# Half-size weight sums on VectorE, ordering ties beside the norm, and spare accumulators for the last projection in a two-layer attention kernel

## The chip, the cores and the metric

The kernel runs on one core of one Trainium2 chip. The metric is the device time of one launch in microseconds (us). The work is split over TensorE (PE, matrix products; PEld is its weight load), VectorE (DVE), ScalarE (ACT), GpSimd (POOL) and DMA queues issued by SyncE (SP), ScalarE and GpSimd.

## The reference

The input x has 8 images of 32 x 32 tokens with 512 channels. Two layers follow each other, each on the group-normalised x (32 groups of 16 channels, statistics over all tokens of an image):

```python
# layer 0: 16 heads of 32
x = x + (softmax(q k^T * 32**-0.5) v) @ w_proj + b_proj     # q, k, v = gn(x) @ w_qkv
# layer 1: 4 heads of 128, with relative position logits
x = x + (softmax(q k^T + rel_w(q) + rel_h(q)) v) @ Wo       # q = gn(x) @ Wq / sqrt(128), k, v = gn(x) @ Wk, Wv
```

All is float32.

## The kernel before

**Layout.** Activations are kept transposed: a `block` is 128 partitions x 4 chunks of channels x 1024 tokens (2 MB), and eight of them exist (`BLOCKS = 8`). Finished residuals are put away in device memory (`put_away`, L228) and fetched again (`fetch`, L235), both on SP's queue.

**Products in seven parts.** Each 512 x 512 projection is done by a scheme with seven half-size products in place of eight. It needs half-size sums of the activations (`forming`, L336 on, the instruction at L360: four VectorE additions s1, s2, a21, s4 of 128 x 1024) and half-size sums of the weights. The weights' sums are made once at run time: `Matrix.fetch` (L138) loads a matrix, `add_up` makes four subtractions of 128 x 512 (L152) and stores them (L154). For the first three matrices this is at the start. `other_sums` does it for the other five during the first pass, all with GpSimd, fetch and store on GpSimd's queue too.

`seven` emits, for one unit (half of the output channels), the products in the order 0, 5, 1, 4, 6, 2, 3 (`ORDER`) on three accumulators x, y, z. A product is 8 matmuls in 32-column strips, 16 records in the trace. Between the products stand the snapshots: `p1` (ScalarE, L406), `a` (VectorE, L411, after product 5), `b` (L419, after product 4), `p7` (ScalarE, L425). Each accumulates further in the same PSUM bank, so the next product into y waits until `a` or `b` is read. `begun` and `half_done` hold the last `a` and `b`. Each accumulator is a `bank` (three buffers in PSUM). A sink takes the results: `Plain` writes them, `Onto` adds them to the residual (VectorE L507, with bias L509, and GpSimd L502). The very last projection (`after_last`) uses `two_first` and `five_last` instead: products 0 and 1 of both units, then the forms, then 5, 4, 6, 2, 3 of each unit.

**Attention of layer 0** (`attention_0`): 64 steps per image, each with a front (scores, L603, into the four-bank tile `ps`; exponential on ScalarE, L611, into one of two `e` buffers) and, one step later, a back (values, L622, into `acc`; VectorE adds e to the running sum, L631 for the first two of a group of eight steps, L633 after that). At the end of a group `finish` sums over partitions on TensorE (L643) and `normalise` divides (ScalarE L566, VectorE L568 to L584, GpSimd L588). Layer 1 (`attention_1`) works on tiles of 512 columns from `bank` (L718, L719, L721, L730, L741).

**Norm.** `statistics` makes two bn_stats (L259) per chunk and one bn_aggr (L260), with two buffers `st`; `group_norm` makes a chain of small VectorE instructions (L285 to L296), a power on GpSimd (L300), and one normalising instruction for each of the four chunks (L304). In the first image the statistics read the SBUF copies that ScalarE makes of the transposed input (L837).

**The passes.** For b = 0 to 8 the attention of layer 0 on image b is emitted side by side with a chain of other work: the output projection `after_0` and norm of image b-1, the output projection `after_1` of image b-2, the projections `second` and attention of layer 1 of image b-1, and the load, norm and projections of image b+1. `side_by_side` hands out products by their cost so that both end together; `woven` puts a step of one generator after every so many of another. In b=0 the chain is the rest of image 0's projections woven with the load of image 1, then image 1's projections woven with `other_sums`. In b=1 it begins with `after_0` of image 0; in b=2 to 7 with `after_0`, then `after_1` woven with the norm. Pass b=8 has no layer 0 attention; after it stands `after_last`.

**Order.** The text's order is a priority. The framework lays out each engine's queue by its own plan of when instructions become ready (in the trace, product 6 of the last projection is issued ahead of product 4). `tc.issue_after(i)` forbids the instructions in its block to stand ahead of i in i's engine's queue. Before the change it ties the norm's first instruction behind `half_done` (b=2 on), its L304 behind `begun` (b=1), and the form additions of a loaded image behind `added`, the last sum of layer 1.

## Time and profile before

| | us |
|---|---|
| median of three runs | 3847.89 (3846.76 to 3849.78) |
| the profiled execution's own time | 3848.35 |
| its span in the trace | 3846.6 |
| TensorE busy in the span | 3789.4 |
| VectorE, ScalarE, GpSimd busy | 2555.1, 1760.2, 621.6 |
| mean granted TensorE clock | 0.998 |

A line of the timeline gives start, duration, engine, source line, operation, output and input tiles with their sizes, the number of instructions merged, and in brackets the idle time of the engine ahead of it and what ended that. A line of the waits gives who waited for whom, the total in us, how many times, and the longest. A matmul's end is modelled: where an engine's instructions overlap, their durations may contain waiting.

### The profile page before, as it was taken

The numbers are of one execution on the slowest core, as the hardware profiler recorded it, in microseconds if no ns is written. First come the engines' busy times: TensorE is split into PE (matmuls) and PEld (weight loads), VectorE is DVE, ScalarE is ACT, GpSimd is POOL, SyncE is SP. The second block draws the span as 40 slices with busy tenths as digits, with TensorE's granted clock in tenths as the row PEclk, the third lists the DMA queues.
The fourth block names the chain that finished last, engine by engine and source line by source line (L and its number), as shares of the span: only waits on it lengthen the run. The fifth ranks groups of instructions, "written<-read, shape, count | busy, mean of one in ns | idle before, by whom it ended". The sixth has DMA issues, their size and how long they took to land.

```text
span 3846.6 us, 79883 instructions
## 1 busy us (share of the span) xinstructions
PE 3789.4 (99%) x34478; PEld 1376.3 (36%) x34478; DVE 2555.1 (66%) x2966; ACT 1760.2 (46%) x1830; POOL 621.6 (16%) x398
## 2 busy tenths in 40 slices
PE   9999999999999999999999999999999999999998
PEld 4222244222443234432343323433234332334353
DVE  6777775686755866558665686656866568665544
ACT  3554544545444454444544445444454445553132
POOL 1342101121011211012101121111210112001201
PEclk9999999999999999999999999999999999999999
DMA  6122120142202322023120241103311023110321
GB/s 185 61 88 81 41 59 6 44 122 62 56 9 83 89 54 56 13 92 85 45 55 16 93 93 38 50 21 98 90 40 41 26 96 78 33 37 31 109 41 26
DMA packets 482983, 234.72 MB, mean 61 GB/s; under 512 B 269600, under 2 KB 461376, under 8 KB 481600
## 3 DMA queue, kind: packets, MB, share of 16 engines
q1 hardware_dynamic: 470992, 213.74, 20.5%
q0 software_dynamic: 2608, 13.70, 1.0%
q8 instruction: 273, 4.47, 0.5%
q10 hardware_dynamic: 9024, 2.10, 0.3%
q14 instruction: 86, 0.70, 0.1%
HBM read 170.72 MB, written 58.72 MB: 60 GB/s over the span
## 4 chain that ended last, share of the span: by engine, by line
PE 88%; DVE 7%; ACT 2%; issue 2%; DMA 0%; SPq 0%; POOL 0%; DVEq 0%; ACTq 0%; POOLq 0%
PE ps L603 12%; PE ps L718 11%; PE acc L730 11%; PE acc L622 11%; PE y_q L327 4%; PE y_v L327 4%; PE y_k L327 4%; PE ps L719 3%; PE x_q L327 3%; PE x_v L327 3%; PE z_k L327 3%; PE x_k L327 3%; PE z_q L327 3%; PE z_v L327 3%; DVE es L633 2%; ACT e L611 2%
## 5 line engine op out<-in xcount | busy, mean ns | idle before, releaser
L611 ACT ACTIVATE e<-ps 128x2048 f32<-128x2048 f32 x512 | 961.7, 1878 | 840.1 <-PE ps L603 630.0
L633 DVE TENSOR_TENSOR es<-es,e 128x2048 f32<-128x2048 f32 x384 | 894.8, 2330 | 403.7 <-ACT e L611 400.4
L603 PE MATMUL ps<-q,k 32*64 32x512 f32 x8192 | 579.1, 614 | 17.1 <-ACT e L611 17.1
L622 PE MATMUL acc<-e,v 128*32 128x512 f32 x4096 | 546.7, 605 | 0.0
L721 ACT ACTIVATE e<-ps 128x512 f32<-128x512 f32 x512 | 305.7, 597 | 507.1 <-PE ps L719 436.4
L718 PE MATMUL ps<-q,k 128*128 128x512 f32 x1024 | 525.0, 594 | 0.2 <-DVE posT L704 0.2
L730 PE MATMUL acc<-e,v 128*128 128x512 f32 x1024 | 522.0, 593 | 0.3 <-ACT e L721 0.3
L588 POOL TENSOR_TENSOR q<-q,su 128x512 f32<-128x512 f32 x128 | 212.7, 1662 | 1550.3 <-DVE su L584 1427.7
L741 DVE TENSOR_TENSOR es<-es,e 128x512 f32<-128x512 f32 x384 | 290.4, 756 | 251.0 <-ACT e L721 248.4
L719 PE MATMUL ps<-posT,sel 128*128 128x512 f32 x512 | 406.6, 794 | 0.0
L718 PEld LDWEIGHTS ps<-q,k 128*128 128x128 f32 x1024 | 192.5, 190 | 230.1 <-issue 218.5
L603 PEld LDWEIGHTS ps<-q,k 32*64 32x64 f32 x8192 | 120.6, 130 | 410.1 <-issue 223.5
L730 PEld LDWEIGHTS acc<-e,v 128*128 128x128 f32 x1024 | 193.1, 189 | 147.3 <-issue 92.6
L622 PEld LDWEIGHTS acc<-e,v 128*32 128x32 f32 x4096 | 81.3, 108 | 412.7 <-issue 366.1
L631 DVE TENSOR_TENSOR es<-e,e 128x2048 f32<-128x2048 f32 x64 | 171.6, 2681 | 32.8 <-ACT e L611 32.7
L568 DVE STREAM_TRANSPOSE tu<-su 128x512 f32<-128x512 f32 x128 | 90.5, 707 | 97.3 <-ACT su L566 95.7
L719 PEld LDWEIGHTS ps<-posT,sel 128*128 128x128 f32 x512 | 97.3, 190 | 122.5 <-issue 122.5
L566 ACT COPY su<-sums 128x512 f32<-128x512 f32 x128 | 74.9, 585 | 131.2 <-PE sums L643 81.5
L704 DVE TENSOR_TENSOR posT<-pp,posT 32x512 fp32r<-32x512 f32 x128 | 112.0, 875 | 31.9 <-ACT posT L699 30.6
L492 POOL TENSOR_TENSOR k<-b_k,p_k 128x512 f32<-128x512 f32 x32 | 52.0, 1624 | 483.4 <-ACT p_k L425 472.7
L699 ACT CAST posT<-pp 32x512 fp32r<-32x512 f32 x128 | 105.9, 827 | 45.8 <-PE pp L686 44.7
L492 POOL TENSOR_TENSOR v<-b_v,p_v 128x512 f32<-128x512 f32 x32 | 51.6, 1614 | 433.9 <-ACT p_v L425 433.9
(214 smaller groups left out, 4546.0 us busy)
## 6 DMA issues: line engine op xcount, KB each, us to landing
w_qkv<-ws_qkv SPq DMA_DIRECT2D x168, 128.0 KB, 2.5
d<-x0T SPq DMA_DIRECT2D x32, 512.0 KB, 3.0
x1T<-d SPq DMA_DIRECT2D x32, 512.0 KB, 5.9
d<-x1T SPq DMA_DIRECT2D x32, 512.0 KB, 3.6
x2T<-d SPq DMA_DIRECT2D x32, 512.0 KB, 6.1
w_qkv<-in_L_conv_w_qkv SPq DMA_DIRECT2D x126, 128.0 KB, 2.2
out<-ot SPq DMA_DIRECT2D x240, 64.0 KB, 2.0
xs<-in_x SPq DMA_DIRECT2D x224, 64.0 KB, 2.5
```

Source lines behind the costliest of these rows:

```text
L327: ins = nc.tensor.matmul(out[columns, :], weights[:, columns], moving, start=start, stop=stop, skip_group_check=open_sum,)
L588: nc.gpsimd.tensor_tensor(dst, dst, su, op=ALU.mult)
L603: nc.tensor.matmul(ps[some, r, :], k[m][rows, j * P + 64 * i : j * P + 64 * i + 64], q[m][rows, h * NB : (h + 1) * NB], start=True, stop=True,
L611: nc.scalar.activation(e, ps, AF.Exp, scale=D0 ** -0.5)
L622: nc.tensor.matmul(acc[r * D0 : (r + 1) * D0, :], v[:, j, c0 : c0 + D0], e[:, r, :], start=(j == blocks[0]), stop=(j == blocks[-1]),)
L631: nc.vector.tensor_add(state["esum"], state["first"], e)
L633: nc.vector.tensor_add(state["esum"], state["esum"], e)
L718: nc.tensor.matmul(ps, k[h][:, keys], q[:, h, queries], start=True, stop=False)
L719: nc.tensor.matmul(ps, sel_flat[:, keys], posT[:, h, queries], start=False, stop=True)
L721: nc.scalar.activation(e, ps, AF.Exp, scale=1.0 / math.sqrt(D1))
L730: nc.tensor.matmul(acc, v[:, j, h * D1 : (h + 1) * D1], e, start=(j == 0), stop=(j == NT - 1),)
L741: added[0] = nc.vector.tensor_add(state["esum"], state["esum"], e)
```

## The change

Seven edits. (1) `other_sums` uses VectorE for all four subtractions of each matrix, one step each, each tied behind `summed`, the last sum of layer 0's attention; fetch and store stay on GpSimd's queue; it is woven with every product instead of every seventh. (2) Image 1's load is woven with every product of `rest_of_first` instead of every second, and its forms are tied behind `summed`. (3) Image 0's `after_0` and the last projection run as `in_two_parts`: products 0 and 1 of both units, with the forms woven between them, then the other five of each unit. (4) In the last projection the second unit's accumulators are the tiles `acc` and `ps` that the attention used. (5) Beside `after_1` and the norm (and beside image 0's `after_0`) each sum of layer 0's attention is tied behind `reader`, the last `a` or `b` of `seven`; the norm's L304 are tied behind `summed`. (6) The statistics of the last image's second unit in `after_0` are emitted with the norm, tied behind `begun`. (7) The first image's statistics read the PSUM banks, into one tile `looks` for all eight.

```diff
         def add_up(self, engines, store, keep=False):
+            run(self.adding(engines, store, lambda: last_form[0], keep))
+        def adding(self, engines, store, behind, keep=False):
...
                 engine = engines[i]
-                with tc.issue_after(last_form[0].ins) if engine is nc.vector else nullcontext():
+                with tc.issue_after(behind().ins) if engine is nc.vector else nullcontext():
                     engine.tensor_tensor(sums[:, i], x, y, op=ALU.subtract)
+                yield 0
             d = dram.tile([P, 4, HC, HN], F32, tag="sums", name=f"ws_{self.name}", bufs=8)
...
+    reader = [None]
+    summed = [None]
+    beside_norm = [False]
...
     def by_columns(out, weights, moving, start, stop, open_sum=False):
...
         a = snapshot("es1", f"a_{name}")
-        begun[0] = nc.vector.tensor_add(a, y, p1)
+        reader[0] = begun[0] = nc.vector.tensor_add(a, y, p1)
         sink.early(p1, a)
...
         b = snapshot("es1", f"b_{name}")
-        half_done[0] = nc.vector.tensor_add(b, y, p1)
+        reader[0] = half_done[0] = nc.vector.tensor_add(b, y, p1)
         sink.middle(b)
...
-    def two_first(fs, u, sink, name):
+    def two_first(fs, u, sink, name, bank=bank):
...
         nc.scalar.copy(p1, x)
+        yield HC
         product(x, 1, False)
         sink.c11(x)
+        yield HC
         return p1
-    def five_last(fs, u, sink, name, p1):
+    def five_last(fs, u, sink, name, p1, bank=bank):
         product = taken(fs, u, False)
...
         a = snapshot("es1", f"a_{name}")
-        nc.vector.tensor_add(a, y, p1)
+        begun[0] = nc.vector.tensor_add(a, y, p1)
         sink.early(p1, a)
+        yield HC
         product(y, 4, False)
         b = snapshot("es1", f"b_{name}")
-        nc.vector.tensor_add(b, y, p1)
+        half_done[0] = nc.vector.tensor_add(b, y, p1)
         sink.middle(b)
+        yield HC
         z = bank(f"z_{name}")
...
         nc.scalar.copy(p7, z)
+        yield HC
         product(y, 2, False)
         sink.c12(y, p1)
+        yield HC
         product(z, 3, False)
...
         sink.c22(b, p7)
+        yield HC
+    def in_two_parts(x, m, sinks, name, room=None, done=lambda u: None, behind=None, banks=(bank, bank)):
+        early = [x[:, :HC, :NB], x[:, HC:, :NB]]
+        p1s, fs = [], []
+        def products():
+            for u in range(2):
+                stream.unit(m, False, u)
+                p1s.append((yield from two_first(early, u, sinks[u], f"{name}_{u}", banks[u])))
+        def sums():
+            fs.extend((yield from forming(x, name, room, behind)))
+        yield from woven(products(), sums(), 0, 1)
+        for u in range(2):
+            stream.unit(m, False, u)
+            yield from five_last(fs, u, sinks[u], f"{name}_{u}", p1s[u], banks[u])
+            done(u)
     class Plain:
...
                 state["esum"] = mem.tile([P, HB, NB], F32, tag="es0", name=f"es_{name}", bufs=1)
-                nc.vector.tensor_add(state["esum"], state["first"], e)
+                other = state["first"]
             elif j != blocks[0]:
-                nc.vector.tensor_add(state["esum"], state["esum"], e)
+                other = state["esum"]
+            if j != blocks[0]:
+                with tc.issue_after(reader[0].ins) if beside_norm[0] else nullcontext():
+                    summed[0] = nc.vector.tensor_add(state["esum"], other, e)
             if j != blocks[-1]:
...
         yield from group_norm(st, xT, f"0_{b}")
-        st["xn"] = yield from forming(x, f"xn0_{b}", behind=lambda: added[0])
+        st["xn"] = yield from forming(x, f"xn0_{b}", behind=lambda: added[0] or summed[0])
     def load_first(st):
...
         xT = chunks(x)
+        st["mv"] = small.tile([P, 32], F32, tag="mv", name="mv_0_0", bufs=2)
+        nc.gpsimd.memset(st["mv"], 0.0)
+        looks = small.tile([P, CC, NH, 6], F32, tag="looks", name="looks")
         for h in range(NH):
...
                 nc.scalar.copy(part, banks[cc])
+                nc.vector.bn_stats(looks[:, cc, h, :], banks[cc])
...
             nc.tensor.matmul(idle[:, t % CC, :], ident, rows[:, t, :], start=True, stop=True)
-        for cc in (0, 2, 1, 3):
-            statistics(st, xT, cc, "0_0")
+        for cc in range(CC):
+            nc.vector.bn_aggr(
+                st["mv"][:, : 2 * CC].rearrange("p (s c) -> p c s", c=CC)[:, cc, :],
+                looks[:, cc].rearrange("p h s -> p (h s)"),
+            )
         st["kept"] = put_away(xT, "0_0")
...
     def after_0(b, st, hook=None):
-        fs = st.pop("ao0") if "ao0" in st else forms(st["q0"], f"ao0_{b}", block(f"forms_{b}"))
         x = st["x1"] = block(f"x1T_{b}")
         xT = fetch(st["kept"], x)
+        sinks = [
+            Onto(halves(xT, u), [bproj_sb[:, n * HC + u : n * HC + u + 1] for n in range(2)])
+            for u in range(2)
+        ]
+        def done(u):
+            def look(u=u):
+                for n in range(2):
+                    statistics(st, xT, n * HC + u, f"1_{b}")
+            if b == B - 1 and u:
+                st["look"] = look
+            else:
+                look()
+        if "ao0" not in st:
+            yield from in_two_parts(
+                st["q0"], WP, sinks, f"wp_{b}", block(f"forms_{b}"), done, lambda: summed[0]
+            )
+            return
+        fs = st.pop("ao0")
         for u in range(2):
-            bias = [bproj_sb[:, n * HC + u : n * HC + u + 1] for n in range(2)]
             stream.unit(WP, False, u)
-            yield from seven(
-                fs, u, False, Onto(halves(xT, u), bias), f"wp_{b}_{u}", hook if u else None
-            )
-            for n in range(2):
-                statistics(st, xT, n * HC + u, f"1_{b}")
+            yield from seven(fs, u, False, sinks[u], f"wp_{b}_{u}", hook if u else None)
+            done(u)
     def norm_1(b, st, after=None, behind=None):
         xT = chunks(st["x1"])
+        if "look" in st:
+            with tc.issue_after(begun[0].ins):
+                st.pop("look")()
         st["kept"] = put_away(xT, f"1_{b}")
...
         sinks = [Onto(halves(xT, u), then=put_out(b, st, xT, u)) for u in range(2)]
-        early = [x[:, :HC, :NB], x[:, HC:, :NB]]
-        p1s = []
-        for u in range(2):
-            stream.unit(WO, False, u)
-            p1s.append(two_first(early, u, sinks[u], f"wo_{b}_{u}"))
-        fs = forms(x, f"ao1_{b}")
-        for u in range(2):
-            stream.unit(WO, False, u)
-            five_last(fs, u, sinks[u], f"wo_{b}_{u}", p1s[u])
+        idle = [psum.tile([P, NB], F32, tag="acc", name="wo_acc", bufs=1)]
+        scores = psum.tile([P, HB, NB], F32, tag="ps", name="wo_ps", bufs=1)
+        idle += [scores[:, r, :] for r in range(HB)]
+        run(in_two_parts(x, WO, sinks, f"wo_{b}", banks=(bank, lambda name: idle.pop(0))))
     def woven(main, side, start, gap, places=(0,)):
...
+    def with_norm(part):
+        beside_norm[0] = True
+        yield from part
+        beside_norm[0] = False
     def marked():
...
     def units(m, rows=False):
...
+    def in_parts(m):
+        return [(m, False, u, some) for some in (FIRST_TWO, LAST_FIVE) for u in range(2)]
...
         if b >= 1:
-            plan += units(WP)
+            plan += units(WP) if b > 1 else in_parts(WP)
         if b == 1:
...
             plan += FIRST if b else units(WQ0) + units(WK0)[:1] + units(WV0, True)
-    plan += [(WO, False, u, some) for some in (FIRST_TWO, LAST_FIVE) for u in range(2)]
+    plan += in_parts(WO)
...
     def other_sums():
...
             m.fetch(nc.gpsimd)
-            m.add_up([nc.gpsimd] * 4, nc.gpsimd)
+            yield from m.adding([nc.vector] * 4, nc.gpsimd, lambda: summed[0])
             yield 0
     def at_once(do):
...
             if past is not None:
-                norm = norm_1(b - 1, last, after=lambda: half_done[0])
+                norm = norm_1(
+                    b - 1, last, after=lambda: half_done[0], behind=lambda: summed[0]
+                )
             else:
                 norm = norm_1(b - 1, last, behind=lambda: begun[0])
-            rest.append(after_0(b - 1, last, forms_past if past is not None else None))
+            first = after_0(b - 1, last, forms_past if past is not None else None)
+            rest.append(first if past is not None else with_norm(first))
             total += PRODUCT
             if past is not None:
-                rest.append(woven(later(after_1, b - 2, past), norm, 3, 3))
+                rest.append(with_norm(woven(later(after_1, b - 2, past), norm, 3, 3)))
                 total += PRODUCT
...
         else:
-            rest.append(woven(rest_of_first(here), incoming, 0, 2))
+            rest.append(woven(rest_of_first(here), incoming, 0, 1))
             total += PRODUCT
...
             before = later(before_0, b + 1, coming, forms_0 if last is not None else None)
-            rest.append(before if last is not None else woven(before, other_sums(), 2, 7))
+            rest.append(before if last is not None else woven(before, other_sums(), 2, 1))
             total += 3 * PRODUCT - PRODUCT // 2
```

## The prediction

> **What bounds the kernel now.** I read the page's busy shares first, then who TensorE waited for, then TensorE's gaps in order of time, then the timeline around each gap.
>
> ```profile
> span 3846.6 us, 79883 instructions
> ...
> PE 3789.4 (99%) x34478; PEld 1376.3 (36%) x34478; DVE 2555.1 (66%) x2966; ACT 1760.2 (46%) x1830; POOL 621.6 (16%) x398
> ```
>
> TensorE is the bound; the change removes no matmul, so it can win only TensorE's idle time, 3846.6 - 3789.4 = 57.2 us, and stretches in which its clock was low or a stall hides inside the modelled busy time. The waits of TensorE (us in total, times, longest):
>
> ```profile
> PE ps L603 <- ACT e L611: 17.1, 16, 2.9
> PE y_wo L327 <- DVE a_wo L411: 9.1, 6, 1.8
> ...
> PE x_v L327 <- issue: 3.5, 1, 3.5
> PE sums L643 <- DVE es L633: 3.1, 2, 1.8
> PE y_wp L327 <- DVE forms L360: 2.5, 1, 2.5
> ```
>
> Laid out in time the gaps are: the start 9.0 (4.8 of it the first input); the pass b=0 9.7; b=1 5.4; b=2 to 6 12.35, the same pair (0.98 and 1.42 to 1.77) in each; b=7 2.7; b=8 1.6 and some of 0.3; six of 0.34; the last projection 2.4, and 10.3 after the last matmul. Now one view of each kind. The pair, in b=2:
>
> ```profile
> 843.11 2.98 DVE L304 TENSOR_SCALAR x1T<-x1T,back,rstd 128x1024 f32<-128x1024 f32 x4 [1.20 <-POOL rstd L300]
> 846.01 2.29 DVE L633 TENSOR_TENSOR es<-es,e 128x2048 f32<-128x2048 f32 x1
> 848.38 1.88 ACT L611 ACTIVATE e<-ps 128x2048 f32<-128x2048 f32 x1 [5.25 <-DVE es L633]
> 850.32 1.12 PE L603 MATMUL ps<-q,k 32*64 32x512 f32 x16 [0.98 <-ACT e L611]
> 854.02 4.64 DVE L633 TENSOR_TENSOR es<-es,e 128x2048 f32<-128x2048 f32 x2
> 858.59 0.68 DVE L411 TENSOR_TENSOR a_wo<-y_wo,p_wo 128x512 f32<-128x512 f32 x1
> 859.32 1.92 PE L327 MATMUL y_wo<-f_ao,w_o 128*32 128x512 f32 x16 [1.42 <-DVE a_wo L411]
> ```
>
> Four normalising instructions in a row hold up a sum whose input was there at 839.44. The exponential waits for the sum (two e buffers), TensorE for the exponential. Later two sums in a row stand ahead of the snapshot a_wo, and the product that goes on in the same PSUM bank waits. The weights, in b=0:
>
> ```profile
> 156.08 9.38 DVE L633 TENSOR_TENSOR es<-es,e 128x2048 f32<-128x2048 f32 x2
> 156.23 3.76 POOL L152 TENSOR_TENSOR prep_q<-prep_q 128x512 f32<-128x512 f32 x3
> 165.60 1.07 PE L643 MATMUL sums<-es,ones 128*32 128x512 f32 x8 [1.82 <-DVE es L633]
> 166.59 1.82 PE L603 MATMUL ps<-q,k 32*64 32x512 f32 x16
> ```
>
> Two sums take 9.38 instead of 4.6 while POOL subtracts; TensorE waits 1.82 and then runs slowly (1.82 for 16 matmuls that take 1.11 elsewhere). The opening of b=1, the start, the last projection:
>
> ```profile
> 326.53 2.94 PE L327 MATMUL y_wp<-forms,w_p 128*32 128x512 f32 x16 [2.50 <-DVE forms L360]
> ```
>
> ```profile
> 11.40 1.29 DVE L259 BATCH_NORM_STATS2 st<-x0T 128x6 f32<-128x512 f32 x2 [1.04 <-ACT x0T L837]
> ```
>
> ```profile
> 3820.29 2.33 PE L327 MATMUL y_wo<-f_ao,w_o 128*32 128x512 f32 x17 [1.01 <-DVE a_wo L453]
> 3832.62 1.92 PE L327 MATMUL y_wo<-f_ao,w_o 128*32 128x512 f32 x16
> ```
>
> [...] a sum (two SBUF inputs) has a median of 2.29 and a longest of 6.08, the latter under POOL's subtractions. [...] Here slow matmuls followed gaps of 1.82 and 2.50 already, and not the one of 2.92 at 141.17; I count slow clock only where the trace has it.
>
> **The change part by part.** Times are of the profiled execution: 3848.35 us, span 3846.6, so 1.75 lie around the span. The median of the three runs shown is 3847.89, 0.46 below.
>
> 1. *First statistics.* Now the two `st` buffers let VectorE take only two of the first half's four statistics; it idles 1.04 until 11.40 and ends the eighth at 15.4. With one tile `looks` all four first-half ones (4 x 0.645 from 9.07) end by 11.65, the others by 14.2, four aggregates (0.2 each) by 15.0, against 15.6. [...] The warming matmuls (5.32) start a little later, as VectorE too must leave their bank; they end by 17, before the product, at 18.9. Next comes POOL's power (1.04), unchanged. Bounds: 0 to -2.5 (the latter if TensorE's cold start, 3.46 for a product of 1.9, shortens too). I take **-0.8**.
>
> 2. *Weights.* POOL's 20 subtractions (five matrices, 42 us of POOL with their contention) leave; VectorE gets 20 of 0.68 (its own L152 rows at the start: 0.678 to 0.683), 13.6 us. They lie in VectorE's idle time of about 0.9 ahead of most sums. A late sum costs TensorE nothing up to 2.45 (one ends at 285.51, the exponential that needs its buffer starts at 287.96). That cover is missing at the seven group ends, where the normalising steps and the first sum already leave gaps of 0.6 to 1.5; two or three subtractions will fall there: +1.5. What goes: the 1.82 at 165.60 and the slow stretch behind it (1.82 - 1.11 and 1.94 - 1.06), 3.4 together. The gap of 2.92 at 141.17 comes from the four form additions crowding before L631; they wait for buffers that the previous products hold, so placing their text earlier frees few of them: -0.9. The POOL queue keeps the fetches and stores, each store now behind VectorE; the first reader of a stored sum came 60 us later. Bounds: -8 (all gaps of b=0) to +10 (below). I take **-2.8**.
>
> 3. *Opening of b=1.* Two products of the second unit (2 x 1.72) move ahead of the forms: they fill the 2.50 and spare the cold rows (2.94 - 1.90 and 1.72 - 1.11): -4.1. The order 5, 4 of the last five puts a product right behind the snapshot it waits for (0.69 and perhaps a sum of 2.29 ahead of it); attention steps lie between most: +0.5. Bounds -5.2 to +1. I take **-3.6**. The 1.85 at 376.34 stays: its norm is still behind `begun`.
>
> 4. *Norm beside the last projection, b=2 to 7.* With the normalising instructions tied behind sums, two at most (1.5 us) stand between two sums instead of four (2.98); the exponential of 848.38 then has its buffer in time: 0.98 goes. With sums tied behind the last snapshot, a_wo runs at about 854.3 to 856.4 rather than 858.59, before the 857.9 at which TensorE wanted it: 1.42 goes. Queued behind a waiting sum: a sum tied to `b` may wait about 1.2 more (VectorE stands until 836.55 instead of starting at 835.36), inside the 2.45. The norm ends later by a sum or two, 5 us; its first reader comes at 863, 17 us on. Of 12.35 I take 10.0 and of b=7 1.3 (the 1.31 at 3214.35): **-11.3**. Bounds 0 to -13.9.
>
> 5. *b=8.* The last unit's statistics (four of 0.64, two aggregates) go behind a_wo, which stood behind three of them: the gap of 1.62 goes, save for the residual additions: **-1.5** (0 to -1.6).
>
> 6. *Last projection.* From 3805.24 to 3836.26 lie 31.0 us for 14 products (24.1) and the sums (0.7): 6.2 waste, of which 2.43 shows as gaps; the rest is y_wo waiting for b_wo (3822.97, 3832.57). With the second unit's three accumulators in the attention's free banks its products can fill the first unit's waits. But the framework's plan may still run the units in turn, and outputs bunch at the end (1 MB per unit; the DMA moved 130 to 150 GB/s there). Bounds -6.2 to +1; I take **-3.0**.
>
> Sum: -0.8 - 2.8 - 3.6 - 11.3 - 1.5 - 3.0 = -23.0; 3848.35 - 23.0 = 3825.35, about **3825**.
>
> **Rivals.** (a) *The ties change little*: each only forbids an instruction to come earlier than another, and the norm's gap moves to another sum. For it: the framework lays every queue anew. Against: the tie names just the two pairs that the trace shows late. Term 4 nil: 3825 + 11.3 = 3836. (b) *VectorE stuck behind a fetch*: POOL waited 5.0 to 5.2 for each of three fetches; in VectorE's queue the same wait, less 2.45 of cover, is 2.7 five times: 3825 + 13.5 = 3838.5. Against it: VectorE waits for no DMA anywhere in the trace of before. (c) *Slower: the sums tied behind snapshots.* Four snapshots in each of six passes, 24 places; if at each the exponential chain is held for a product (1.72), TensorE loses 41 and term 4 gives nothing: 3836 + 41 = 3877. It ends slower once each place loses 0.8 (11.7 and the 7.7 of the bound, over 24). Against: the cover of 2.45, and in these passes two products often stand between attention steps, which lengthens it.
>
> **Chances.** A measurement of this kernel can tell about 0.2%, 7.7 us. Forecast 0.62, its own range 3814 to 3834 (all of 4 and 6 won: 3848 - 34; half of 4 and none of 6: 3834); (a) 0.17; (b) 0.12; (c) 0.06; no net change 0.03. Faster (below 3840): 0.62, 0.15 of (a), 0.08 of (b): 0.85. Slower: (c) and a little: 0.07. Same: 0.08. The range 3813 to 3840 holds the forecast and most of (a) and (b).
>
> **What would show it.** In TensorE's waits: a_wo L411 from 9.1 to under 2, L603 on the exponential from 17.1 to about 9, y_wp on the forms gone, sums on es L633 nil; the waits of y_wo at the end shrink, and the last projection takes TensorE some 28 us instead of 31.0. Wrong: VectorE waiting for a prep fetch; new gaps at L603 in b=2 to 7; the second unit's products at the end still in turn.

## The result, and the profile after

| | before | after |
|---|---|---|
| median | 3848.07 us (3846.54 to 3850.42, 22 runs) | 3854.30 us (3852.28 to 3855.52, 22 runs) |
| ratio after/before | | 1.0016, 95% interval 1.0010 to 1.0021 |
| profiled execution, its span | 3848.35, 3846.6 | 3855.17, 3853.4 |

The forecast was 3825; the kernel became 6.2 us slower. Medians are of fast executions; of the six of e8 below, one that took 5572.67 us at a mean granted clock of 0.65 is left out. The page of the kernel after, span and busy shares:

```profile
span 3853.4 us, 79904 instructions
...
PE 3790.3 (98%) x34478; PEld 1371.9 (36%) x34478; DVE 2573.4 (67%) x2986; ACT 1762.4 (46%) x1830; POOL 609.0 (16%) x378
```

TensorE's matmuls are the same 34478; its idle time is 63.1 us instead of 57.2. The waits of TensorE in the kernel after (us in total, times, longest):

```profile
PE ps L637 <- ACT e L645: 26.0, 22, 4.2
PE idle L883 <- DVE looks L879: 5.5, 1, 5.5
...
PE y_wp L335 <- DVE a_wp L463: 2.6, 2, 1.8
PE y_v L335 <- DVE a_v L419: 2.1, 1, 2.1
...
PE y_k L335 <- DVE b_k L427: 1.5, 1, 1.5
...
PE wo_ps L335 <- DVE x2T L541: 0.8, 1, 0.8
...
PE y_wo L335 <- DVE a_wo L419: 0.7, 1, 0.7
```

The waits for a_wo in passes 2 to 6 are gone as predicted (9.1 to 0.7; of the 9.1, 1.6 lay in b=8, and the 0.7 lies there too). But the scores wait longer for the exponential (17.1 to 26.0), and several waits are new: the warming matmuls wait for the looks (the first image's statistics), y_v at the start, y_k in b=0 and y_wp in the opening of b=1 wait for snapshots, and the tile wo_ps, in which the accumulators y and z of the last projection's second unit are two banks, waits for three different readers. To see where the time went I laid the starts of the same TensorE instruction side by side in both timelines, and took the lengths between them:

| stretch (us) | before | after | kept parts (e11) |
|---|---|---|---|
| start to first score matmul | 60.03 | 62.60 | 59.19 |
| to image 0's x_wp (pass b=0) | 248.50 | 256.08 | 246.87 |
| to second layer's x_q (opening of b=1) | 84.44 | 82.91 | 82.92 |
| to last projection's x_wo (rest of b=1 to b=8) | 3412.27 | 3407.33 | 3407.17 |
| last projection, to the end of its last matmul | 31.02 | 34.22 | 31.03 |

So 2.6 are lost at the start, 7.6 in b=0 and 3.2 in the last projection; 1.5 and 4.9 are won between. The last column is explained below. Three stretches of the timeline of the kernel after show the three losses. The start, first before, then after:

```profile
8.45 2.05 ACT L837 COPY x0T<-turned 128x512 f32<-128x512 f32 x4 [4.54 <-PE turned L830]
```

```profile
8.40 0.59 ACT L878 COPY x0T<-turned 128x512 f32<-128x512 f32 x1 [4.46 <-PE turned L871]
9.02 0.70 DVE L879 BATCH_NORM_STATS2 looks<-turned 128x6 f32<-128x512 f32 x1 [4.66 <-ACT x0T L878]
10.70 3.13 ACT L878 COPY x0T<-turned 128x512 f32<-128x512 f32 x6 [1.71 <-PE turned L871]
15.04 0.59 ACT L878 COPY x0T<-turned 128x512 f32<-128x512 f32 x1 [1.21 <-DVE looks L879]
15.65 0.70 DVE L879 BATCH_NORM_STATS2 looks<-turned 128x6 f32<-128x512 f32 x1 [0.27 <-ACT x0T L878]
16.50 7.26 PE L883 MATMUL idle<-x_rows,ident 128*128 128x512 f32 x12 [5.51 <-DVE looks L879]
```

Before, ScalarE copied all four first-half chunks in a row (2.05 us from 8.45). Now it copies one and then stands: each further copy from the same four-bank tile waits until VectorE has looked at the bank before (those at 13.24 and 15.04 start when looks have ended at 13.21 and 15.00), and the queue has copies of the second half, which wait for TensorE until 10.70, in between. The last copy of the tile waits 1.21 for a look, and its own look ends at 16.35; only then can the warming matmuls have the tile. They run at a granted clock of 0.50 until 20.3, and the product x_v starts at 23.69 (19.74 before). The granted clock is 1.00 then and the product takes 1.93 instead of 3.46 (before, it lay mostly in a stretch at 0.50, from 20.09 to 23.51), so that of the 3.9 a loss of 2.6 is left at the first score matmul. Pass b=0:

```profile
256.66 0.58 POOL L158 DMA_DIRECT2D ws_v<-prep_v  x1 [17.67 <-DVE prep_v L155]
261.65 0.59 ACT L516 COPY v<-x_v 128x512 f32<-128x512 f32 x1 [5.38 <-DMA ws_v<-prep_v]
264.07 2.01 PE L637 MATMUL ps<-q,k 32*64 32x512 f32 x16 [4.17 <-ACT e L645]
```

The fourth matrix had its block since 207; its subtractions came one by one until 256.4, its store landed 4.8 us later, and image 1's values need that block. ScalarE stands 5.38 in the copy that writes them, with the exponential queued behind it, and the sixteen matmuls of TensorE after the gap take 2.01 instead of 1.11. Of the 7.6, some 1.7 (an estimate: one spell of 3.41 us at 0.50) are a second fall of the clock, from 146.56 to 149.97. Such a second fall comes only in some executions: the same pass took 254.0 to 255.4 in e1 to e4 and e8, whose edits don't touch it, and 256.7 and 257.0 in e17 and e18. The last projection, second unit:

```profile
3835.81 1.92 PE L335 MATMUL wo_ps<-q,w_o 128*32 128x512 f32 x16 [0.81 <-DVE b_wo L468]
3838.49 1.92 PE L335 MATMUL wo_ps<-f_wo,w_o 128*32 128x512 f32 x16 [0.75 <-ACT p_wo L474]
3841.22 1.92 PE L335 MATMUL wo_ps<-q,w_o 128*32 128x512 f32 x16 [0.81 <-DVE x2T L541]
```

Product 6 (3835.81) writes bank z, and waits for a reader of y; product 2 (3838.49) writes y and waits for a reader of z; product 3 writes z and waits for a reader of y. Before, product 6 ran inside the waits of y.

### The profile page after: what moved, and what is told of

Same layout as the page of the kernel before. It is cut to its first block, busy times and chain, and to the rows that moved or that the text cites. A ratio compares the mean times of both kernels' runs of the same rounds, so it can differ in the third digit from the quotient of the medians.

```text
span 3853.4 us, 79904 instructions
## 1 busy us (share of the span) xinstructions
PE 3790.3 (98%) x34478; PEld 1371.9 (36%) x34478; DVE 2573.4 (67%) x2986; ACT 1762.4 (46%) x1830; POOL 609.0 (16%) x378
## 4 chain that ended last, share of the span: by engine, by line
PE 89%; DVE 7%; ACT 3%; issue 1%; DMA 1%; POOL 0%; SPq 0%; ACTq 0%; DVEq 0%; POOLq 0%
PE ps L637 12%; PE acc L656 11%; PE ps L756 11%; PE acc L768 11%; PE y_k L335 4%; PE y_v L335 4%; PE y_q L335 4%; PE ps L757 3%; PE z_k L335 3%; PE z_q L335 3%; PE x_v L335 3%; PE x_k L335 3%; PE x_q L335 3%; PE z_v L335 3%; DVE es L671 2%; ACT e L645 2%
## 5 line engine op out<-in xcount | busy, mean ns | idle before, releaser
L622 POOL TENSOR_TENSOR q<-q,su 128x512 f32<-128x512 f32 x128 | 200.1, 1563 | 1528.7 <-DVE su L618 1391.6
```

The costliest lines, as they stand in the source:

```text
L622: nc.gpsimd.tensor_tensor(dst, dst, su, op=ALU.mult)
```

## The experiments

Theory: (i) accesses of different engines to different banks of one PSUM tile are made to wait for each other; this costs 2.6 at the start and 3.2 at the end. (ii) A matrix whose sums come late holds a block, and what waits for the block stalls; 6 us in b=0. (iii) Beside the norm VectorE is full, so a wait of TensorE that is taken away there comes back later. Rivals are in each expectation. The kernel before, timed again beside each kernel, took 3847.5 to 3848.0. Where nothing else is said, an experiment is an edit of the changed kernel, called after (3854.3); line numbers in profiles are those of the kernel shown.

**e1, e2: the first statistics.** e1 puts the old code back, e2 is this edit of after:

```diff
-                nc.vector.bn_stats(looks[:, cc, h, :], banks[cc])
+                nc.vector.bn_stats(looks[:, cc, h, :], part)
```

> The changed kernel with only the first statistics put back (read from the SBUF copies, two st buffers). Theory: the copies on ScalarE and the statistics on VectorE take turns on the one four-bank tile, which put the warming matmuls at 16.50 and the first score matmul at 62.60 us instead of 60.03. So the first score matmul comes back to 60.0 and the time is 3854.3 - 2.6 = 3851.7. Rival (a late start is made up later, since the weights and the load of image 1 decide the first pass): first score matmul at 60.0, but 3854.3 all the same.

> The changed kernel with the one tile for all eight looks kept, but each statistic reading the SBUF copy, not the PSUM tile. Theory (the turns on one PSUM tile are the loss, and the two st buffers were a real limit): no turns, the four first-half statistics run in a row, the chain after them starts at about 15.0 instead of 16.63 (15.65 in the kernel before); first score matmul at 59 to 60, time 3851 to 3851.7. Rival (the st buffers were no limit; VectorE is only as early as ScalarE's last copy): the chain starts at 15.6 as in the kernel before, 3851.7. Rival (the reading from PSUM was not the cause): 3854.

Measured: e1 3855.08 (ratio to before 1.0018, 1.0012 to 1.0025), e2 3853.80 (1.0016, 1.0009 to 1.0022). No gain in either median. In the profile of e2 the first score matmul starts at 58.77, earlier than in both kernels, and that execution took 3849.5; in e1's profile it starts at 62.55 although the queues up to there are those of the kernel before, since TensorE ran at a clock of 0.55 from 20 to 30 us (0.83 before). This is taken up again at e13, e17 and e18.

**e3, e4: the last projection.** e3 takes the three common banks for both units (`run(in_two_parts(x, WO, sinks, f"wo_{b}"))`), e4 only separates the tiles:

```diff
         scores = psum.tile([P, HB, NB], F32, tag="ps", name="wo_ps", bufs=1)
-        idle += [scores[:, r, :] for r in range(HB)]
-        run(in_two_parts(x, WO, sinks, f"wo_{b}", banks=(bank, lambda name: idle.pop(0))))
+        idle += [scores[:, 0, :]]
+        run(
+            in_two_parts(
+                x, WO, sinks, f"wo_{b}", banks=(bank, lambda name: idle.pop(0) if idle else bank(name))
+            )
+        )
```

> The changed kernel with the second unit of the last projection back in the three common banks; the generator in two parts stays. Theory: the last projection (first x_wo matmul to the end of the last matmul) takes 31.0 instead of 34.2 us, time 3854.3 - 3.1 = 3851.2. Rival (the new generator's order, not the accumulators, costs the 3.1): 34 us and 3854.

> The changed kernel with the second unit's three accumulators in three different tiles: x in acc, y in one bank of ps, z in a common bank. No accumulator shares a tile with another. Theory (readers and writers of different banks of one tile are made to wait for each other): the product 6 fills the wait for a and the product 3 that for the last addition again; last projection 28 to 31 us, time 3848.5 to 3851.2. Rival (the units standing in turn is what costs, whatever the tiles): 33 to 34 us, about 3854.

Measured: e3 3850.22 (1.0008, 1.0000 to 1.0016), e4 3850.86 (1.0009, 1.0001 to 1.0018); the last projection takes 31.04 in both. In e4's timeline product 6 (z_wo) runs between the matmuls of product 4 again:

```profile
3829.60 0.61 PE L335 MATMUL wo_ps<-f_wo,w_o 128*32 128x512 f32 x3
3830.02 1.46 PE L335 MATMUL z_wo<-q,w_o 128*32 128x512 f32 x10
```

This settles (i) for the end: one tile costs 3.2. It also shows that free accumulators gain nothing over the common banks: the units still stand one after the other, 31.04 against 31.02.

**e5, e6: the weights.** e5 has GpSimd and one matrix per seven products as before; e6 keeps VectorE, with two empty steps after each matrix. First e5, then e6:

```diff
-            yield from m.adding([nc.vector] * 4, nc.gpsimd, lambda: summed[0])
+            m.add_up([nc.gpsimd] * 4, nc.gpsimd)
...
-            rest.append(before if last is not None else woven(before, other_sums(), 2, 1))
+            rest.append(before if last is not None else woven(before, other_sums(), 2, 7))
```

```diff
             yield from m.adding([nc.vector] * 4, nc.gpsimd, lambda: summed[0])
             yield 0
+            yield 0
+            yield 0
```

> The changed kernel with the weights' sums as before: GpSimd subtracts, one matrix after every seventh product. Theory (the new pace lets the fourth matrix take a block ahead of image 1's values, and ScalarE's copy of those waits 5.4 us for its store): the gap of 4.17 at 264 and the slow clock behind it go, the gap of 1.82 and the slow stretch of the kernel before come back at about 165; from the first score matmul to the first x_wp 248.5 to 250 instead of 254.4 to 256.1; time 3854.3 - 6 = 3848.3. Rival (the loss in the first pass lies in the denser load of image 1, which stays): 254 to 256 again, 3854.

> The changed kernel with VectorE still subtracting one by one behind additions, but with two empty steps after each matrix, so that one matrix is fetched per seven products as before, not per five. Theory (the block taken early is the loss, VectorE's subtractions are not): ScalarE waits for no store of weights, no gap of 4 us at 264; first score matmul to first x_wp 248 to 250; time 3854.3 - 6 = 3848.3, equal to GpSimd's version or up to 1.5 below it. Rival (the 13.6 us of subtractions on VectorE are the loss, whatever the pace): 253 to 256, 3852 to 3854, and GpSimd's version faster by 3 or more.

Measured: e5 3848.26 (1.0001, 0.9993 to 1.0010), with 249.56 from the first score matmul to x_wp; e6 3850.73 (1.0007, 0.9999 to 1.0015), with 247.91 there, the shortest so far. So the pace cost, not VectorE's 13.6 us. But e6 loses 3 us in the opening of b=1 (85.93), by the same mechanism one block later. Its timeline:

```profile
326.14 1.27 POOL L536 TENSOR_TENSOR x1T<-x1T,p_wp 128x512 f32<-128x512 f32 x1 [10.34 <-DMA x1T<-d]
328.69 2.28 DVE L368 TENSOR_TENSOR forms<-q 128x1024 f32<-128x1024 f32 x1 [3.26 <-POOL q L622]
338.05 2.02 PE L637 MATMUL ps<-q,k 32*64 32x512 f32 x16 [3.38 <-ACT e L645]
```

and SP's own wait there:

```profile
SPq L239 <- DMA ws_o<-prep_o: 3.6, 1, 3.6
```

The last subtraction of the fifth matrix ran at 314.24, its store was issued at 315.22, and the fetch of x1T, which waited 3.6 for that store, at 319.85. GpSimd's gather (L536, its addition to the residual) waits for the fetch, the division by the sums (L622) stands behind it, the forms behind that, a sum behind the forms. With e15 below this settles (ii).

**e7, e8: the ties.** e7 is the kernel before with the ties of passes 2 to 7 alone (its last projection is written in two parts on the common banks, and takes 31.02 as before); e8 is after without the normalising tie:

```diff
-                norm = norm_1(
-                    b - 1, last, after=lambda: half_done[0], behind=lambda: summed[0]
-                )
+                norm = norm_1(b - 1, last, after=lambda: half_done[0])
```

> The kernel before with the ties beside the norm and the second layer's output projection alone (passes b=2 to 7). The prediction's step 4 gives 3847.6 - 11.3 = 3836.3. Theory now (VectorE has no idle time left in these 40 us, so a wait that is removed comes back at the end of the group; the changed kernel gained 0.9 in each of b=2 to 6): 3847.6 - 4.7 = 3842.9, with a new gap of about 1.3 at the third scores after each pair. Rival (the changed kernel's gain there is owed to other edits, the ties alone give nothing): 3847.6.

> The changed kernel without the tie of the normalising instructions behind the last sum; the sums stay tied behind the snapshots. Theory (VectorE is full here; the order only moves the wait): four normalising instructions in a row again, a gap of about 1 ahead of a score matmul, less of the gap of 1.26 later; each pass within 0.5 of the changed kernel, 3852 to 3856.5. Rival of the prediction (the tie itself removes 0.98 in each pass and costs nothing elsewhere): 0.98 more in each of five or six passes, 3859 to 3860.

Measured: e7 3843.47 (0.9989, 0.9982 to 0.9995), -4.4, as theory (iii) had it and not -11.3. e8 3862.81 (1.0039, 1.0026 to 1.0052; five executions, 3861.67 to 3863.54), 8.5 above after: outside what I expected, on the rival's side. What the tie does is seen in pass b=2; first the kernel after:

```profile
845.48 1.12 PE L637 MATMUL ps<-q,k 32*64 32x512 f32 x16 [0.44 <-ACT e L645]
853.81 1.53 DVE L308 TENSOR_SCALAR x1T<-x1T,back,rstd 128x1024 f32<-128x1024 f32 x2 [0.31 <-POOL rstd L304]
884.59 1.12 PE L637 MATMUL ps<-q,k 32*64 32x512 f32 x16 [1.26 <-ACT e L645]
```

and e8:

```profile
849.94 1.54 DVE L308 TENSOR_SCALAR x1T<-x1T,back,rstd 128x1024 f32<-128x1024 f32 x2 [1.20 <-POOL rstd L304]
883.52 1.12 PE L637 MATMUL ps<-q,k 32*64 32x512 f32 x16 [1.98 <-ACT e L645]
```

In both, one gap of the pair is gone and the other is down to 0.44, and a third has come 40 us later, where the first sum of the next group stands behind four form additions and the division. In after, from 845.1 to 886.8, VectorE is busy for 40.91 of 41.70. The tie lets a sum run while GpSimd makes the power, so VectorE idles 0.31 there, not 1.20: 0.89 won. One pass (from one group end to the same one a pass later) takes 471.2 in before, 470.3 in after and in e7, 471.2 in e8. TensorE won just what VectorE's idle time lost. That is 0.9 in each of five passes. The rest of e8's loss lies elsewhere: pass b=4 takes 472.9 because the clock stood at 0.50 for 3.41 us from 1827.43, behind the same gap of 1.98, and b=7 is 2.4 longer, with a gap of 1.92 ahead of the sums' matmuls that the kernel after has not. Why it comes stays open.

**e9, e10: VectorE's load beside the norm.** Of e7, passes 2 to 8. e9 leaves out two of the four normalising instructions (half the channels stay as they are); e10 gives them to ScalarE:

```diff
+        on_scalar = (1, 3) if behind is not None and after is not None else ()
+        if on_scalar:
+            shift = small.tile([P, CC], F32, tag="shift", name=f"shift_{name}")
+            nc.vector.scalar_tensor_tensor(shift, mean, -1.0, rstd, op0=ALU.mult, op1=ALU.mult)
...
+            if cc in on_scalar:
+                nc.scalar.activation(
+                    xT[cc],
+                    xT[cc],
+                    AF.Identity,
+                    bias=shift[:, cc : cc + 1],
+                    scale=rstd[:, cc : cc + 1],
+                )
+                yield 0
+                continue
```

> The ties alone (3843.5), and in the passes b=2 to 8 two of the four normalising instructions of the second layer's norm are left out: half of its channels stay as they are. This takes 2 x 0.74 us from VectorE in each pass and nothing from TensorE. Theory (VectorE is full for some 40 us beside the norm, 40.9 of 41.7 us busy, so TensorE's gap there is VectorE's work over TensorE's): the gap of 1.25 at the end of the group goes, and about 1.3 in each of b=2 to 7: 3843.5 - 7 = 3836.5. Rival (the gap comes from the order at the end of the group, four form additions ahead of the first sum, whatever went before): the gap stays at 1.25, 3843.

> The ties alone (3843.5), with two of the four normalising instructions of b=2 to 8 moved to ScalarE (scale and bias; one more small instruction on VectorE makes the bias, about 0.2). ScalarE is busy for 19.5 of these 41.6 us. Theory (VectorE is full, ScalarE isn't): VectorE loses 1.3 us, the gap of 1.25 shrinks below 0.3, 3843.5 - 6 = 3837.5. Rival (an instruction of about 1 us on ScalarE stands ahead of an exponential and TensorE waits for that instead): a new gap of about 1 at the scores beside the norm, 3843 to 3849.

Measured: e9 3840.79 (0.9982, 0.9974 to 0.9990), 2.7 below e7, not 7. The timeline of e9, b=2:

```profile
851.21 3.01 DVE L674 TENSOR_TENSOR es<-es,e 128x2048 f32<-128x2048 f32 x1
875.75 1.12 PE L640 MATMUL ps<-q,k 32*64 32x512 f32 x16 [0.90 <-ACT e L648]
```

Of the 1.49 left out, a sum that now falls together with GpSimd's gather took 0.76 back (3.01; 2.25 in e7), and VectorE waited 0.27 for TensorE elsewhere. From the snapshot b to the first sum of the group it took 34.15 instead of 34.52, 0.37 less; TensorE's gap fell by 0.35. So (iii) holds in its exchange of one for one, and my size was wrong: TensorE got back only a part of the work that was taken out of the full queue, 0.35 of 1.49. e10 was slower, 3852.71 (1.0014, 1.0008 to 1.0021), as its rival said. ScalarE's and TensorE's lines in b=2:

```profile
841.68 1.24 ACT L312 ACTIVATE x1T<-x1T,shift,rstd 128x1024 f32<-128x1024 f32 x1 [3.45 <-DVE shift L309]
843.45 1.92 PE L349 MATMUL z_wo<-q,w_o 128*32 128x512 f32 x16 [0.79 <-ACT p_wo L447]
846.35 1.12 PE L651 MATMUL ps<-q,k 32*64 32x512 f32 x16 [0.98 <-ACT e L659]
```

A copy of an accumulator and an exponential stand behind 1.24 each. ScalarE, busy 46% of the span, has no slack at this place. Not all of the loss is ScalarE's: the small VectorE instruction that makes the bias (L309) is not tied, so the sum stands behind it and VectorE idles 1.20 for the power again, which the tie had cut to 0.31. A version with that instruction tied was not run.

**e11, e12: the parts that gained.** e11 is after with e5's weights, the old load of image 1, e2's looks and e4's tiles; e12 adds e10's edit.

> The parts of the change that gained or were mended: the ties, image 0's output projection in two parts, the last image's late statistics, the last projection with three separate tiles, the looks from the SBUF copies; the weights' sums on GpSimd and the load of image 1 as before. If the parts add up as the single runs give them: 3848.3 (the changed kernel with the weights back) - 3.4 (separate tiles) - 0.5 to 2.6 (statistics) = 3842.3 to 3844.4. Rival (the two-part opening of b=1 costs what it gains, and the tie's 0.9 per pass is all there is): equal to the ties alone, 3843.5.

> The same with two of the normalising instructions of b=2 to 8 on ScalarE. Theory: the gains add, 3843.3 - 6 = 3837. Rival (ScalarE is late instead): not below the version without it.

Measured: e11 3839.10 (0.9978, 0.9969 to 0.9987), below both kernels and below what I had added up; e12 3849.07 (1.0004, 0.9996 to 1.0012), 10 worse, as e10 was.

**e13 to e16: one part of the change back into e11.** e13: looks from PSUM; e14: image 1's load with every product (`woven(rest_of_first(here), incoming, 0, 1)` for `0, 2`), its forms tied; e15: VectorE's subtractions, all four in one step at the old pace (`run(m.adding([nc.vector] * 4, ...))`); e16: the old opening of b=1.

> The kept parts (3839.1), with the looks reading the PSUM tiles again, as in the change. Theory (the start costs what the first landmark shows): first score matmul at 62.5 instead of 59.2, 3839.1 + 3.4 = 3842.5. Rival (putting the statistics back into the whole change moved its median by -0.5 and +0.8 only, so the start is made up later): 3839 to 3839.6.

> The kept parts (3839.1) with image 1's load woven with every product and its forms tied behind the last sum, as in the change. Theory (the fall from the changed kernel with the weights back, 3848.3, to the kept parts is 9.2, of which separate tiles give 3.4 and the start 3.4, so 2.4 is the denser load's): first score matmul to first x_wp 249.5 instead of 246.9, 3841.5. Rival (the denser load costs nothing): 3839.

> The kept parts (3839.1), with the four subtractions of each matrix on VectorE, all four in one step at the old pace, tied behind the last sum. Theory (what cost was the block held by a matrix whose sums come late, one by one; GpSimd's contention costs 1 to 2 in the first pass): no wait of 3 us or more for a store of weights, the 1.82 type of gap gone, 3837.5 to 3839. Rival (20 subtractions of 0.68 on VectorE delay its sums, wherever they are put): 3841 to 3845.

> The kept parts (3839.1) with the opening of b=1 as in the kernel before: forms first, then each unit's seven products, no ties there. The prediction's step 3 gives 3839.1 + 3.6 = 3842.7. Theory from the traces (the two gaps of 0.81 and 1.77 behind the snapshots of the second unit take back half): 3839.1 + 1.6 = 3840.7. Rival (nothing): 3839.

| | median us | above e11 | ratio to before | from the landmarks of its profile |
|---|---|---|---|---|
| e13 | 3844.91 | 5.8 | 0.9990 (0.9982 to 0.9999) | start +3.9, b=0 +0.5, b=1 +1.7 |
| e14 | 3841.20 | 2.1 | 0.9983 (0.9977 to 0.9990) | start -0.2, b=0 +1.9, b=1 +1.7 |
| e15 | 3839.99 | 0.9 | 0.9981 (0.9973 to 0.9988) | start -0.5, b=0 +0.7 |
| e16 | 3840.92 | 1.8 | 0.9982 (0.9975 to 0.9989) | b=1 +1.5 |

The statistics do cost: 5.8 against the same looks from the SBUF copies, 3.9 of it at the start. The two-part opening is worth 1.5 to 1.8. VectorE's and GpSimd's sums can't be told apart at the old pace (the 0.9 of e15 lies within the noise), which again says that the pace cost. The +1.7 of e13 and e14 in b=1 is slow clock: the product behind the unchanged gap of 1.77 takes 3.62 and 3.60 instead of 1.92. The denser load came out 2 slower, but how much of that is its own is not shown: it turns the gap of 2.92 into 1.52 (y_k waiting for b_k) and 1.83, and the rest of e14's gaps is one of 1.81 ahead of the sums' matmuls at 166.00, of a kind that comes and goes with the old load too (before has it, e11 has not).

All profiles together show the start better than one or two do. The first score matmul starts at 62.4 to 63.1 in the seven with looks from PSUM (after, e3 to e6, e8, e13), at 60.0 to 61.0 in five of the six with the old statistics (before, e7, e9, e10, e18; the sixth is e1 with 62.55), and at 58.7 to 59.2 in the seven with one tile and SBUF copies (e2, e11, e12, e14 to e17).

**e17, e18: second profiles of e2 and e1.** One run each.

> A second profile of the changed kernel with the looks from the SBUF copies, whose first profile (3849.5) lay 4.3 below its own median (3853.8). Theory (after a gap of 1.8 to 4.2 the clock falls in some executions and not in others): the order and the gaps are the same as in the first profile, and the longer time shows as slow matmuls behind the gaps at 18.5, 141, 258 or 357 us: one or two of the windows there with a granted clock below 0.9 that had 1.00 before. Rival (the time goes into waits, so that a part of the gain is really made up later): longer gaps at full clock.

> A second profile of the changed kernel with the first statistics put back (first profile 3855.8, median 3855.1, lowest 3850.4). Theory: the same gaps; which of the four places runs slowly differs from the first profile (there 20 to 30 us at a clock of 0.50 to 0.59, 3.01 behind the gap of 1.77), and the sum of the slow places accounts for the difference in time to within 1 us. Rival: different gaps.

Measured: 3856.34 and 3856.41. First e2's timeline, then that of e17, the same kernel:

```profile
237.61 1.12 PE L637 MATMUL ps<-q,k 32*64 32x512 f32 x16 [2.02 <-ACT e L645]
357.71 1.92 PE L335 MATMUL y_wp<-forms,w_p 128*32 128x512 f32 x16 [1.77 <-DVE a_wp L463]
```

```profile
237.76 1.91 PE L637 MATMUL ps<-q,k 32*64 32x512 f32 x16 [2.03 <-ACT e L645]
360.51 3.38 PE L335 MATMUL y_wp<-forms,w_p 128*32 128x512 f32 x16 [1.76 <-DVE a_wp L463]
```

The gaps are equal to 0.01; what differs is the matmul behind them. By the landmarks e17 is 2.7 longer in b=0 and 3.3 in b=1, and equal elsewhere to 0.1 (6.1 in all at the last matmul, spans 6.9 apart). e18 keeps e1's gaps too: 2.2 better at the start, 1.5 worse in b=0, 1.7 worse in b=1. So no wait makes the start's gain up again.

The profile's record of the granted clock shows which gap is followed by slow clock. In all 20 profiles, from the first full clock to the last matmul, low clock (0.50) lasts 3.41 us or a multiple of it, and within one execution all such spells start on one grid of 3.413 us: in after at 13.44, 146.56 and 262.61, which are 39 and 34 steps apart. Where the grid lies differs from execution to execution. Below are two grid steps around the gap of 1.77, first of e17, then of e2: the stretch, its length, TensorE's busy time, and, third from the end, the granted clock.

```profile
357.42:360.83 3.41, 1.65 (x14) 0.36 (x14) 3.00 (x4) 0.00 (x0) 0.30 (x1) 1.00 0.54 192
360.83:364.24 3.41, 3.41 (x21) 0.75 (x18) 0.31 (x1) 0.00 (x0) 0.97 (x1) 0.50 0.02 5
```

```profile
353.61:357.02 3.41, 2.34 (x22) 0.33 (x10) 3.34 (x5) 0.60 (x1) 0.00 (x0) 1.00 0.54 189
357.02:360.43 3.41, 2.72 (x26) 0.63 (x26) 1.33 (x3) 0.00 (x0) 1.28 (x1) 1.00 0.03 8
```

In e17 the gap lies whole in one step, and the next step is slow; in e2 an edge of the grid cuts it, and none is. Of the 14 profiles with this gap, the product behind it is slow in five (e1, e13, e14, e17, e18), where the gap lies whole in one step and begins 0.9 us or more into it; it is fast in four where an edge cuts the gap and in five where it begins in the first 0.5 us of a step. Over all 20 profiles, between 25 and 3800 us and outside slow spells, all 21 steps in which TensorE idled 2.0 us or more were followed by a slow one, 12 of the 37 with 1.76 to 2.0, and none with less.

What remains open is why the medians of e1 and e2 hide the start's gain: whether their grid lies badly more often than that of after can't be told from two profiles of each. Warming that runs right up to the first product doesn't decide it, for the product behind 1.77 is fast in e2, e11 and e15 (1.92 in each), which lack it, and slow in e13 (3.62), which has it.

## Why the prediction was wrong, step by step

Terms 1, 2 and 6 came out with the wrong sign, and 3, 4 and 5 gave half of what was forecast or less.

1. *First statistics: forecast -0.8; +2.6 in the profile.* The step "all four first-half ones (4 x 0.645 from 9.07) end by 11.65" failed. It is not the single instruction that failed: the eight that read PSUM in after (L879) took 0.68 to 0.70, the eight that read the SBUF copies in before (L259) 0.64 to 0.70; the step's 0.645 is half of a pair's 1.29. I ordered the copies and looks bank by bank (an assumption; the trace of before has no such pair), while they take turns over the whole four-bank tile: the order is kept between banks of one tile, by waits in the program's own queues (ScalarE 1.21 for a look ahead of the tile's last copy, TensorE 5.51 for the looks ahead of the warming matmuls). I also wrote that the warming matmuls "end by 17, before the product": they ended at 23.7 and the product waited. The part that I credited to the single tile `looks` is real: with looks at the SBUF copies the product x_v starts at 18.48 (e2) and 18.90 (e11), 19.74 before. How much of the loss is the taking of turns, and how much the longer hold on the tile by the looks themselves, is argued from the timeline; a start with a tile for each bank was not run. In the whole change the medians of e1 and e2 show no gain from mending it; only e13 does.
2. *Weights: forecast -2.8; measured +6.0 (after against e5).* The cover "the first reader of a stored sum came 60 us later" was the failed term: I asked who reads the sums, not who wants the block. The bound of +10 held the size. The stall at 165.60 did go in after, but at the old pace VectorE's sums are no faster than GpSimd's (e15). Of the denser load, priced at -0.9 for the crowding near 141, that gap did fall from 2.92 to 1.84; the wait of y_k for b_k (1.52 at 133.10), for which I had no term, took it back.
3. *Opening of b=1: forecast -3.6; -1.5 in the profile, 1.8 in e16.* The mechanism was right, and the wait of y_wp for the forms is gone. The mis-sized term is the order 5, 4, "+0.5": it shows as gaps of 0.81 and 1.77 ahead of y_wp, 2.6 in all, and can cost a slow product besides.
4. *Beside the norm: forecast -11.3; -4.8 in the profile, -4.4 in e7.* The named gaps went (0.98 to 0.44, 1.42 to nothing), and the step that failed is "its first reader comes at 863, 17 us on": I treated the gaps as faults of order with cover behind them. VectorE had no cover; 0.9 in each pass is its idle time of 1.20, which stands in the first line of the pair that I quoted, becoming 0.31, and the rest returned as the gap of 1.26. e7, e8 and e9 agree on this exchange.
5. *b=8: forecast -1.5; measured -0.2* (307.83 to 307.59 from the sums at 3325.63 to x_k). The gap of 1.62 went, but two of 0.47 and 0.69 came some 8 and 12 us later, in the projection's second unit:

```profile
3587.36 1.92 PE L335 MATMUL y_wo<-f_ao,w_o 128*32 128x512 f32 x16 [0.47 <-DVE x2T L541]
3591.69 1.93 PE L335 MATMUL y_wo<-f_ao,w_o 128*32 128x512 f32 x16 [0.69 <-DVE a_wo L419]
```

There a residual addition and the snapshot a_wo stand behind normalising instructions (0.81 from 3585.90 and 2.49 from 3587.23). What failed is the step from "go behind a_wo" to "the gap of 1.62 goes": I asked what stands ahead of one snapshot, not what the norm would next stand ahead of.

6. *Last projection: forecast -3.0; +3.2.* The bound "+1" was too narrow, because it took the banks of one tile as independent accumulators. "The framework's plan may still run the units in turn" was right: even with separate tiles nothing is gained (e4).

The stretches come to 2.6 + 7.6 - 1.5 - 4.8 - 0.2 + 3.2 = 6.9 against 6.8 in the spans. The lower edge of the range, 3814, does not follow from the sum beside it: with all of 4 and 6 won the terms come to -28.8, about 3820. Of the rivals, (a) was half right for term 4: the gap did move to another sum, but because VectorE is full; (b) named the right traffic and the wrong engine: VectorE waits for no fetch of weights, ScalarE waits for a store; (c) shows in no trace here.

## What to carry to other kernels

A buffer that is handed to slow side work is on the clock of whoever needs it next: when the pace of the side work changes, ask for the next owner of each buffer, not only for the reader of the result. Count a multi-bank PSUM tile as one object when several engines touch it, and give accumulators that shall overlap tiles of their own (here 34.22 with y and z in one tile, 31.04 with a tile for each). Where one engine is busy for 98% of a stretch, compare its idle time there with the gap that is to go: here the smaller of the two, 0.9 of 2.4, was what reordering won.

## What the runs showed of the hardware

The granted clock falls behind short gaps, and not in every execution: after the same gap of 1.77 a product took 1.92 in some runs and 3.01 to 3.62 in others; after 2.02 (e2) and 2.03 (e17) sixteen matmuls took 1.12 and 1.91. In all 20 profiles the slow spells start on a grid of 3.413 us, and, counted as above, a step in which TensorE idled 2.0 us or more was followed by a slow one in all 21 cases, one with 1.76 to 2.0 in 12 of 37, one with less in none. A fall to 0.50 costs up to 1.7 us for one step and 3.4 for two (an estimate: half of 3.41 and of 6.83), so single profiles of this kernel can't be compared to better than that, and removing a gap can be worth more than its length (behind the gap of 1.76 in e17 the product took 3.38, 1.46 more than in e2). ScalarE took 1.24 for scale and bias on 128x1024 (e10), against a median of 0.81 and a shortest of 0.73 for the same work on VectorE (after, L308). And a sum on VectorE that started 0.41 into a gather on GpSimd took 3.01 in e9, against 2.25 for the same sum in e7, where the gather was all but over; that returned half of what e9 had taken away. Where the gather started after the sum (0.16, e9), the sum took 2.27 and the gather 3.27, where the one ahead took 1.28.
